# An edge pass re-cut as a pipeline of nine turns, with nine buffers of gathered rows

## The chip, the cores and the metric

The kernel runs on one core of a Trainium2 chip. The metric is device time in microseconds from one launch to its end; the time before is the median of three runs, 9715.59 us (9711.79 to 9739.76). One core has several engines that run their own instruction streams side by side and wait for one another through semaphores: TensorE (PE, matrix products and transposes), VectorE (DVE), ScalarE (ACT), GpSimd (POOL, which here issues the indirect gathers) and SyncE (SP, which here issues plain loads). Matrix products land in PSUM; everything else of the kernel's working data lies in SBUF.

## What is computed

Two graph layers, each added to its input and normalized. There are 12,500 nodes with 64 features and 400,000 edges, sorted by their target node. The first layer takes means over neighbours twice. The second, which the change touches, turns each edge's 64 attributes into a weight vector by two small linear maps with a softplus after each, multiplies it with the row of the edge's source node, and sums over the edges of each target:

```python
def _L1_gnn_ref(node_feats_in, edge_feats, src, dst, Wn, bn, We1, be1, We2, be2, Wc, bc, Wp, bp):
    LOG2 = float(np.log(2.0))
    def ssp(x):
        return jax.nn.softplus(x) - LOG2
    V = node_feats_in.shape[0]
    h = node_feats_in @ Wn.T + bn
    h_src = h[src]
    w = ssp(edge_feats @ We1.T + be1)
    w = ssp(w @ We2.T + be2)
    m = h_src * w
    agg = jax.ops.segment_sum(m, dst, num_segments=V)
    out = ssp(agg @ Wc.T + bc)
    return out @ Wp.T + bp
...
x = _layernorm(x + _L0_gnn_ref(x, edge_index, ...), axis=-1)
x = _layernorm(x + _L1_gnn_ref(x, edge_attr_64, src, dst, ...), axis=-1)
```

## The kernel before

The kernel runs in stages, one after the other: two passes over the edges for the first layer (up to about 4,400 us in the profile), small per-node networks, then **pass three** for the second layer (about 4,690 to 9,385 us), then the last per-node networks. The change touches pass three only.

Pass three cuts the 400,000 edges into 391 groups: 390 of 1,024 edges (T = 8 slots of 128 edges) and a last one of five slots. The loop over windows at L888 runs once on this data. What one group needs, by the names that the profile shows:

- `got`: the source nodes' rows, 64 floats each. `gather` (L849) has GpSimd issue eight indirect gathers (L853) of 128 rows. A buffer of `got` holds one group; there are eight.
- `att`: the edges' attributes, 256 KB, loaded by SyncE (L931) into one of four buffers. TensorE turns them by four transposes into `m_t` (PSUM, L935), ScalarE copies that to `m_at` (L937).
- First map: TensorE `m_1` (L954; the profile calls both maps' results `m`). VectorE adds the bias and clips into `m_v` (`under`, L911), ScalarE takes Exp and Ln (L915, L916), VectorE takes the larger of that and the unclipped value (`larger`, L919).
- Second map: TensorE `m_2` (L948), and the same chain again into `m_w`.
- TensorE turns `m_w` back by four transposes into `m_b` (L941), VectorE multiplies with the gathered rows into `m_m` (L944). This is the last reader of the group's `got` buffer.
- VectorE makes `same` (L860), a 0/1 matrix that says which of 128 neighbouring target nodes each edge belongs to; TensorE sums with it over the edges into `p_sum` (eight products, L868); VectorE adds `p_sum` into its place in `acc` (L886), at an address loaded into a register.

The program is written out in full for all groups; the order in which the groups' steps stand in it is the order in which each engine runs them. Before, it is a pipeline of three groups: in step k the newest group k is gathered, turned and put through the first map, group k−1 goes through the second map and `compare`, and group k−2 is turned back, multiplied, summed and placed:

```python
new = groups[k] if k < len(groups) else None
mid = groups[k - 1] if 0 < k <= len(groups) else None
old = groups[k - 2] if k > 1 else None
```

So within one step, work goes from TensorE to the other engines and back several times: `m_t` to `m_at` to `m_1` to `m_v`, for instance, all belong to one step of one group. The multiply of group k−2 frees the buffer into which group k+6 is gathered. In PSUM, `p_sum` has two buffers, and `m_t`, `m_b`, `m_1`, `m_2` have one each. `same` and `got` live in the pool "esb" (L839), `p_sum` in "eps", the rest in pools that `message_pools` makes (L894).

Of the kernel before, what the change touches and what calls it, by code (L numbers as in the profile page):

```python
# [9 lines left out]
F32 = mybir.dt.float32  # L10
# [40 lines left out]
T = 8  # L51
ET = P * T
W = 128
NG = E // ET
# [13 lines left out]
def gnn_kernel(ctx, tc, x, src, dst, ea, W_lin, b_lin, W1_agg, W1_root, b1, W2_agg, W2_root, b2,  # L68
               Wn, bn, We1, be1, We2, be2, Wc, bc, Wp, bp, out):
    nc = tc.nc  # L70
# [13 lines left out]
    ident = const.tile([P, P], F32, name="ident")  # L84
# [5 lines left out]
    with tc.tile_pool(name="ints", bufs=1) as sb:  # L90
        n = sb.tile([P, KB * P + DW], I32, name="n")
# [5 lines left out]
    eps = const.tile([P, 1], F32, name="eps")  # L97
# [23 lines left out]
    turned = []  # L121
    with tc.tile_pool(name="wps", bufs=2, space=PSUM) as wps, tc.tile_pool(name="given", bufs=1) as given_:
        for w, name in ((Wn, "wn"), (We1, "we1"), (We2, "we2"), (Wc, "wc"), (Wp, "wp")):
            given = diagonal([(0, 0, w)], F, name + "_given", given_)
            pt = wps.tile([P, P], F32, name="pt")
            nc.tensor.transpose(pt, given, ident)
            t = const.tile([P, P], F32, name=name)
            nc.vector.tensor_copy(t, pt)
            turned.append(t)
    wn, we1, we2, wc, wp = turned  # L130
# [19 lines left out]
    be1_c, be2_c = less_log2(column(be1, "be1_c")), less_log2(column(be2, "be2_c"))  # L150
# [73 lines left out]
    with tc.tile_pool(name="prep", bufs=1) as sb, tc.tile_pool(name="prepps", bufs=1, space=PSUM) as ps:  # L224
# [10 lines left out]
        with tc.tile_pool(name="ints2", bufs=1) as sb2:  # L235
            n = sb2.tile([TP, TJ], I32, name="n")
            nc.gpsimd.iota(n, pattern=[[1, TJ]], base=0, channel_multiplier=TJ)
            nc.vector.tensor_scalar(real, n, float(DT), None, op0=ALU.is_lt)
            n = sb2.tile([P, NB], I32, name="n_ids")
# [45 lines left out]
        start = sb.tile([P, NGG + 1], F32, name="start")  # L285
# [15 lines left out]
        g = sb.tile([P, (NGG + 1) * T], I32, name="g")  # L301
# [71 lines left out]
    with tc.tile_pool(name="n0", bufs=2) as sb, tc.tile_pool(name="n0x", bufs=1) as sx, \  # L373
# [3 lines left out]
        for c in range(NCH):  # L377
            cs = slice(c * CH, (c + 1) * CH)
            k = CH // 2
            xt = pairs_turned(ps, sb, xs[:, cs, :].rearrange("p (k j) f -> p k (j f)", j=2), k, P, "xt")  # L380
            ph = ps.tile([P, 1024], F32, name="ph")
            for b, m in banks(k):
                nc.tensor.matmul(ph[:, b * P:(b + m) * P], wlin, xt[:, b * P:(b + m) * P],
                                 start=True, stop=True)
# [3 lines left out]
            for j in range(k):  # L388
                nc.tensor.matmul(py[:, j * 4 * H:(j + 1) * 4 * H], ht[:, j * P:(j + 1) * P], w1,
                                 start=True, stop=True)  # L390
# [332 lines left out]
    with tc.tile_pool(name="n1", bufs=2) as sb:  # L723
        for c in range(NCH):
# [5 lines left out]
            m = sb.tile([P, CH, H], F32, name="m1")  # L730
            nc.vector.tensor_tensor(m, s[:, :, :H], rdeg[:, cs].unsqueeze(2).to_broadcast([P, CH, H]),
                                    op=ALU.mult)
# [15 lines left out]
    with tc.tile_pool(name="n2", bufs=2) as sb, tc.tile_pool(name="n2ps", bufs=1, space=PSUM) as ps, \  # L748
# [33 lines left out]
        for c in range(NCH):  # L782
            cs = slice(c * CH, (c + 1) * CH)
            k = CH // 2
# [34 lines left out]
    windows = nc.values_load(count[0:1, 0:1], min_val=1, max_val=N // W + 1)  # L819


    big = ctx.enter_context(tc.tile_pool(name="big", bufs=1))
    cps = ctx.enter_context(tc.tile_pool(name="cps", bufs=1, space=PSUM))
    acc = big.tile([F, NA], F32, name="acc")
# [4 lines left out]
    e_att = ea[:NG * ET, :].rearrange("(g p t) f -> g p t f", p=P, t=T)  # L829
    l_att = ea[NG * ET:, :].rearrange("(p t) f -> p t f", t=TL)  # L830

    def edge_pass(stages, pools):

        nc.vector.memset(acc, 0.0)
        nc.vector.tensor_copy(base, first)
        with ExitStack() as st:
            sb = st.enter_context(tc.tile_pool(name="esb", bufs=3))  # L839
            ps = st.enter_context(tc.tile_pool(name="eps", bufs=2, space=PSUM))  # L840
            work = pools(st)
            at = {}

            class Group:
                def __init__(self, g):
                    self.g, self.n = g, T if g < NG else TL
                    self.got = None

                def gather(self):  # L849
                    self.got = sb.tile([P, T, F], F32, name="got", bufs=8)  # L850
                    for t in range(self.n):
                        c = self.g * T + t
                        nc.gpsimd.indirect_dma_start(  # L853
                            out=self.got[:, t, :], out_offset=None, in_=t3[:, :],
                            in_offset=bass.IndirectOffsetOnAxis(ap=srcs[:, c:c + 1], axis=0))

                def compare(self):
                    n = self.n
                    self.same = sb.tile([P, T, W], F32, name="same")
                    nc.vector.tensor_tensor(  # L860
                        self.same[:, :n, :], across(steps[:, :W], [P, n, W]),
                        rel[:, self.g * T:self.g * T + n].unsqueeze(2).to_broadcast([P, n, W]),
                        op=ALU.is_equal)

                def gathered_sum(self, m):
                    self.p = ps.tile([F, W], F32, name="p_sum")
                    for t in range(self.n):
                        nc.tensor.matmul(self.p, m[:, t, :], self.same[:, t, :],  # L868
                                         start=t == 0, stop=t == self.n - 1)

                def place(self):
                    g = self.g
                    if g % 8 == 0:
                        k = min(8, NG + 1 - g)
                        loads, v = nc.values_load_multi_w_load_instructions(
                            base_i[0:1, g:g + k], engines=(mybir.EngineType.DVE,), min_val=0, max_val=NP,
                            skip_runtime_bounds_check_because="a base is a node's number, held at NP or "
                            "less where it moves, and acc has W columns more", bass_reorder=False)
                        at.update({g + i: v[i] for i in range(k)})
                        if g:  # L880
                            for load in loads:
                                tc.add_manual_dep(load.ins, at["last"].ins.name, mybir.DependencyInfo(
                                    mybir.DependencyClass.NoSync, mybir.DependencyReason.DATA),
                                    reason="in order")
                    here = acc[:, ds(at[g], W)]
                    at["last"] = nc.vector.tensor_tensor(here, self.p, here, op=ALU.add)  # L886

            with tc.For_i(0, windows, 1):  # L888
                nc.vector.tensor_copy(base_i, base[0:1, :])
                stages(work, [Group(g) for g in range(NG + 1)])  # L890
                nc.vector.tensor_scalar(base, base, float(W), float(NP), op0=ALU.add, op1=ALU.min)
                nc.vector.tensor_scalar(rel, rel, -float(W), None, op0=ALU.add)

    def message_pools(st):  # L894
        return (st.enter_context(tc.tile_pool(name="msb", bufs=2)),
                st.enter_context(tc.tile_pool(name="mps", bufs=1, space=PSUM)))

    def log_part(sb, v, bias, w, name):

# [3 lines left out]
        nc.scalar.activation(a[:, :w], a[:, :w], AF.Ln, bias=half)  # L903
        return a[:, :w]

    def second(work, groups):
        sb, ps = work

        def under(g, p, bias, name):
            a = sb.tile([P, 512], F32, name=name)  # L910
            nc.vector.tensor_scalar(a, p, bias, TOP, op0=ALU.add, op1=ALU.min)  # L911
            return a

        def logs(a):
            nc.scalar.activation(a, a, AF.Exp)  # L915
            nc.scalar.activation(a, a, AF.Ln, bias=half)  # L916

        def larger(a, p, bias):
            nc.vector.scalar_tensor_tensor(a, p, bias, a, op0=ALU.add, op1=ALU.max)  # L919

        nc.scalar.preload_act_table_set("natural_log_exp_and_others")
        for k in range(len(groups) + 2):
            new = groups[k] if k < len(groups) else None
            mid = groups[k - 1] if 0 < k <= len(groups) else None
            old = groups[k - 2] if k > 1 else None
            if new:
                new.gather()
                new.att = sb.tile([P, T, F], F32, name="att", bufs=4)
                if new.n < T:
                    nc.gpsimd.memset(new.att, 0.0)  # L930
                nc.sync.dma_start(new.att[:, :new.n, :], e_att[new.g] if new.g < NG else l_att)  # L931
                pt = ps.tile([P, 512], F32, name="m_t")
                flat = new.att.rearrange("p t f -> p (t f)")
                for j in range(0, 512, P):
                    nc.tensor.transpose(pt[:, j:j + P], flat[:, j:j + P], ident)  # L935
                at = sb.tile([P, 512], F32, name="m_at")
                nc.scalar.copy(at, pt)  # L937
            if old:
                pb = ps.tile([P, 512], F32, name="m_b")
                for j in range(0, 512, P):  # L940
                    nc.tensor.transpose(pb[:, j:j + P], old.w[:, j:j + P], ident)  # L941
                n = old.n
                old.m = sb.tile([P, T, F], F32, name="m_m")
                nc.vector.tensor_tensor(old.m[:, :n, :], pb.rearrange("p (t f) -> p t f", f=F)[:, :n, :],  # L944
                                        old.got[:, :n, :], op=ALU.mult)
            if mid:
                mid.p2 = ps.tile([P, 512], F32, name="m_2")
                nc.tensor.matmul(mid.p2, we2, mid.v, start=True, stop=True)  # L948
                mid.w = under(mid, mid.p2, be2_c, "m_w")
                logs(mid.w)  # L950
                mid.compare()
            if new:
                new.p1 = ps.tile([P, 512], F32, name="m_1")
                nc.tensor.matmul(new.p1, we1, at, start=True, stop=True)  # L954
                new.v = under(new, new.p1, be1_c, "m_v")
            if mid:
                larger(mid.w, mid.p2, be2_c)
            if new:
                logs(new.v)
                larger(new.v, new.p1, be1_c)  # L960
            if old:
                old.gathered_sum(old.m)
                old.place()

    edge_pass(second, message_pools)


    def store(c, y):
# [69 lines left out]
```

## Time and profile before

| | us |
|---|---|
| median of three runs (lowest, highest) | 9715.59 (9711.79, 9739.76) |
| the profiled execution's own time | 9518.89 |
| its span, first to last instruction | 9517.1 |
| mean granted TensorE clock, share of full speed | 0.682 |

The page's busy time by engine, and the costliest group on ScalarE in pass three:

```profile
PE 5181.2 (54%) x28141; PEld 2897.6 (30%) x28141; DVE 4064.2 (43%) x11900; ACT 2257.4 (24%) x3480; POOL 5264.9 (55%) x5503
...
L915 ACT ACTIVATE m_w<-m_w 128x512 f32<-128x512 f32 x391 | 246.3, 630 | 3085.0 <-DVE m_w L911 2680.9
```

In the first line each engine has its busy microseconds, their share of the span and its number of instructions; PEld is the loading of weights into TensorE, which overlaps its products. In the second, a line of the page's list of groups: line, engine, operation, output and input, how many; then busy us in total, mean ns of one, and the idle time of the engine just before them, with what ended most of it. ScalarE's 3,085 us of idle time there say only that ScalarE has little to do; what matters is whose idle time sets the pace. "remote" as a releaser means that the page found no instruction that ended the wait, and "issue" that nothing shown was waited for. Durations of matrix products on TensorE are modelled, not observed to their end.

### The profile page before, as it was taken

The page shows a single profiled execution, that of the slowest core. Times are in us where ns is not written, and L with a number is a line of the kernel's source. Part 1 is how long each engine was busy: PE and PEld are TensorE (multiplying, and loading weights), DVE is VectorE, ACT ScalarE, POOL GpSimd, SP SyncE. Part 2 cuts the span into 40 slices and gives each one's busy share as a digit, 9 for nine tenths or more (in the row PEclk, how much of TensorE's full clock was granted, in tenths as well). Part 3 has the DMA queues.
Part 4 walks back from the last instruction along what each step waited for, and adds up shares of the span by engine and source line. Part 5 has one row for each costly group of instructions (what it writes and reads, how often), then busy time and mean ns, then how long its engine had stood idle before and what let it go on. Part 6 is the DMA issues. An engine that isn't in the chain of part 4 may idle for free.

```text
span 9517.1 us, 85323 instructions
## 1 busy us (share of the span) xinstructions
PE 5181.2 (54%) x28141; PEld 2897.6 (30%) x28141; DVE 4064.2 (43%) x11900; ACT 2257.4 (24%) x3480; POOL 5264.9 (55%) x5503
## 2 busy tenths in 40 slices
PE   2677777777723334344445555555555555555555
PEld 1233333333312222223323333333333333333333
DVE  2566667667611111111533444444344444444445
ACT  0333334334300000000122222222222222222224
POOL 0555455555266555654266666666666666666661
PEclk9566566666655555556567777777777777777777
DMA  2233333333343434344211111111111111111110
GB/s 46 92 119 118 118 118 118 118 118 123 136 153 123 143 134 158 133 161 164 66 38 44 45 45 45 45 45 46 45 45 44 44 46 45 44 45 45 45 45 25
DMA packets 403898, 791.32 MB, mean 83 GB/s; under 512 B 149567, under 2 KB 193439, under 8 KB 403197
## 3 DMA queue, kind: packets, MB, share of 16 engines
q1 hardware_dynamic: 207737, 632.94, 18.3%
q0 software_dynamic: 176032, 143.83, 8.2%
q10 hardware_dynamic: 19653, 8.71, 0.4%
q8 instruction: 237, 3.88, 0.2%
q14 instruction: 239, 1.96, 0.1%
HBM read 516.47 MB, written 268.57 MB: 82 GB/s over the span
## 4 chain that ended last, share of the span: by engine, by line
another core or an unknown queue 15%; PE 11%; issue 10%; DVE 8%; POOL 4%; ACT 3%; DMA 1%; DVEq 0%; POOLq 0%; ACTq 0%
POOL got L853 4%; PE m L948 4%; PE p_sum L868 2%; PE m L954 2%; DVE m_v L919 2%; DVE m_m L944 1%; DVE same L860 1%; ACT m_w L915 1%; DVE m_w L911 1%; DMA got<-t,srcs 1%; ACT m_at L937 1%; ACT m_w L916 1%; DVE m_w L919 1%; PE m_b L941 1%
## 5 line engine op out<-in xcount | busy, mean ns | idle before, releaser
L853 POOL DMA_INDIRECT got<-t,srcs x3125 | 2960.7, 947 | 1888.8 <-issue 819.8
L436 POOL DMA_INDIRECT got<-sent,gidx x2346 | 2277.4, 971 | 1862.8 <-PE p_got L450 850.0
L948 PE MATMUL m<-m_v,we 128*128 128x512 f32 x782 | 629.5, 898 | 1543.0 <-DVE m_v L919 1149.3
L516 PE MATMUL p_counts<-to,lo 128*128 128x392 bf16 x2560 | 1028.9, 463 | 503.4 <-DVE to L515 220.0
L525 PE MATMUL p_sums<-counts,addends 128*64 128x256 bf16 x7840 | 1078.5, 368 | 369.2 <-issue 273.3
L518 ACT CAST counts<-p_counts 128x784 bf16<-128x784 f32 x1120 | 890.8, 813 | 1157.4 <-PE p_counts L516 668.2
L868 PE MATMUL p_sum<-same,m_m 128*64 128x128 f32 x6250 | 923.5, 310 | 281.6 <-DVE m_m L944 281.5
L868 PEld LDWEIGHTS p_sum<-same,m_m 128*64 128x64 f32 x6250 | 820.4, 159 | 731.8 <-DVE m_m L944 491.6
L915 ACT ACTIVATE m_w<-m_w 128x512 f32<-128x512 f32 x391 | 246.3, 630 | 3085.0 <-DVE m_w L911 2680.9
L450 PE MATMUL p_got<-got,same 128*128 128x51 bf16 x4692 | 434.3, 215 | 890.5 <-DVE s_new L417 545.5
L515 DVE TENSOR_SCALAR to<-ramp,keys 128x392 bf16<-128x392 f16 x2560 | 828.0, 323 | 1.8 <-DVE lo L513 1.3
L525 PEld LDWEIGHTS <-addends 128*64 128x64 bf16 x7840 | 525.2, 137 | 829.1 <-issue 716.2
L886 DVE TENSOR_TENSOR acc<-p_sum,acc 64x128 f32 x391 | 109.9, 281 | 1439.7 <-remote 1310.1
L513 DVE TENSOR_SCALAR lo<-ramp,keys 128x128 bf16<-128x128 f16 x2560 | 651.3, 254 | 165.5 <-PE p_counts L516 74.5
L948 PEld LDWEIGHTS m<-m_v,we 128*128 128x128 f32 x782 | 157.5, 251 | 1630.2 <-DVE m_v L919 1203.5
L417 DVE TENSOR_REDUCE s_new<-p_got 128x34 f32<-128x102 f32 x294 | 77.5, 264 | 1324.2 <-remote 969.6
L450 PEld LDWEIGHTS <-same 128*128 128x128 bf16 x4692 | 286.7, 112 | 1100.8 <-issue 656.9
L516 PEld LDWEIGHTS <-lo 128*128 128x128 bf16 x2560 | 271.0, 107 | 1054.3 <-DVE to L515 512.7
L944 DVE TENSOR_TENSOR m_m<-m_b,got 128x512 f32<-128x512 f32 x391 | 267.3, 684 | 747.4 <-remote 395.7
L954 PE MATMUL m<-m_at,we 128*128 128x512 f32 x782 | 577.8, 832 | 0.7 <-ACT m_at L937 0.7
L444 DVE TENSOR_SCALAR same<-ramp,grel 128x256 bf16<-128x256 f16 x2346 | 518.0, 296 | 139.7 <-remote 127.2
L601 ACT COPY rs<-p_sums 128x256 f32<-128x256 f32 x80 | 29.9, 373 | 1980.2 <-PE p_sums L525 958.5
(258 smaller groups left out, 5235.7 us busy)
## 6 DMA issues: line engine op xcount, KB each, us to landing
kept<-counts SPq DMA_DIRECT2D x280, 896.0 KB
counts<-kept SPq DMA_DIRECT2D x560, 448.0 KB
att<-in_edge_attr_dram SPq DMA_DIRECT2D x390, 256.0 KB
got<-t,srcs POOLq DMA_INDIRECT x3125
got<-sent,gidx POOLq DMA_INDIRECT x2346
t<-h SPq DMA_DIRECT2D x7, 448.0 KB
xs<-in_x_dram ACTq DMA_DIRECT2D x6, 448.0 KB
xs<-in_x_dram SPq DMA_DIRECT2D x6, 448.0 KB
```

Of the source, the lines that this page charges most:

```text
L436: nc.gpsimd.indirect_dma_start(out=got[i][:, t, :], out_offset=None, in_=sent[step][:, :], in_offset=bass.IndirectOffsetOnAxis(ap=gidx[:, ...
L444: nc.vector.tensor_scalar(same[:, t, :], ramp[:, :KG * P], grel[:, i * T + t:i * T + t + 1], None, op0=ALU.is_equal)
L450: nc.tensor.matmul(p[:, k * SW:(k + 1) * SW], same[:, t, k * P:(k + 1) * P], rows[:, t, :SW], start=t == 0, stop=t == n - 1)
L513: nc.vector.tensor_scalar(lo, ramp[:, :P], keys[:, 1, i:i + 1], None, op0=ALU.is_equal)
L515: nc.vector.tensor_scalar(to, ramp[:, :MW], keys[:, 0, i:i + 1], None, op0=ALU.is_equal)
L516: nc.tensor.matmul(p[:, k, :MW], lo, to, start=True, stop=True)
L518: copy(counts[:, :, q * 2 * DW:(q + 1) * 2 * DW].rearrange("p h (k d) -> p h k d", k=2), p[:, :, :MW].rearrange("p k (d h) -> p h k d", h= ...
L525: nc.tensor.matmul(p[r:r + YW, :HI * DW], addends[:, h, :], counts[:, h - of, :], start=h < 2, stop=h >= NPP - 2)
L853: nc.gpsimd.indirect_dma_start(out=self.got[:, t, :], out_offset=None, in_=t3[:, :], in_offset=bass.IndirectOffsetOnAxis(ap=srcs[:, c:c + ...
L868: nc.tensor.matmul(self.p, m[:, t, :], self.same[:, t, :], start=t == 0, stop=t == self.n - 1)
L948: nc.tensor.matmul(mid.p2, we2, mid.v, start=True, stop=True)
L954: nc.tensor.matmul(new.p1, we1, at, start=True, stop=True)
```

## The change

Pass three is written as a pipeline of nine turns. In turn k the helper `at(back)` gives group k − back, or nothing at the ends, and each turn does one step for each of nine groups: gathers and the first transposes for group k, the copy and the first map for k−1, the chain after the first map for k−2, the second map for k−3, the chain after it for k−4, the transposes back for k−5, the multiply for k−6, `compare` and the sums for k−7, and `place` for k−8. Attributes are loaded two turns ahead of use. In the text of a turn the steps of ScalarE and VectorE stand ahead of those of TensorE. There are eight turns more than groups, where there were two.

Buffers: `got` nine instead of eight; `att` five instead of four; `same` two instead of three; the `m_...` tiles in SBUF three instead of two; in PSUM `m_1` and `m_2` two instead of one, `p_sum` one instead of two. The number and the shapes of the instructions per group stay as they are.

```diff
-    def edge_pass(stages, pools):
+    def edge_pass(stages):
...
-            ps = st.enter_context(tc.tile_pool(name="eps", bufs=2, space=PSUM))
-            work = pools(st)
+            ps = st.enter_context(tc.tile_pool(name="eps", bufs=1, space=PSUM))
...
-                    self.got = sb.tile([P, T, F], F32, name="got", bufs=8)
+                    self.got = sb.tile([P, T, F], F32, name="got", bufs=9)
...
-                    self.same = sb.tile([P, T, W], F32, name="same")
+                    self.same = sb.tile([P, T, W], F32, name="same", bufs=2)
...
-    def message_pools(st):
-        return (st.enter_context(tc.tile_pool(name="msb", bufs=2)),
-                st.enter_context(tc.tile_pool(name="mps", bufs=1, space=PSUM)))
...
+        def turned(p, a):
+            for j in range(0, 512, P):
+                nc.tensor.transpose(p[:, j:j + P], a[:, j:j + P], ident)
+
+        def attributes(g):
+            g.att = sb.tile([P, T, F], F32, name="att", bufs=5)
+            if g.n < T:
+                nc.gpsimd.memset(g.att, 0.0)
+            nc.sync.dma_start(g.att[:, :g.n, :], e_att[g.g] if g.g < NG else l_att)
+
+        def multiply(g):
+            n = g.n
+            g.m = sb.tile([P, T, F], F32, name="m_m")
+            nc.vector.tensor_tensor(g.m[:, :n, :], g.pb.rearrange("p (t f) -> p t f", f=F)[:, :n, :],
+                                    g.got[:, :n, :], op=ALU.mult)
...
-        for k in range(len(groups) + 2):
...
+        for g in groups[:2]:
+            attributes(g)
+        for k in range(len(groups) + 8):
+            def at(back):
+                return groups[k - back] if 0 <= k - back < len(groups) else None
+            if g := at(0):
+                g.gather()
+            if g := at(-2):
+                attributes(g)
+            if g := at(1):
+                g.at = sb.tile([P, 512], F32, name="m_at")
+                nc.scalar.copy(g.at, g.pt)
+            if g := at(2):
+                g.v = under(g.p1, be1_c, "m_v")
+                logs(g.v)
+            if g := at(6):
+                multiply(g)
+            if g := at(4):
+                g.w = under(g.p2, be2_c, "m_w")
+                logs(g.w)
+            if g := at(8):
+                g.place()
+            if g := at(7):
+                g.compare()
+            if g := at(2):
+                larger(g.v, g.p1, be1_c)
+            if g := at(4):
+                larger(g.w, g.p2, be2_c)
+            if g := at(3):
+                g.p2 = ps.tile([P, 512], F32, name="m_2", bufs=2)
+                nc.tensor.matmul(g.p2, we2, g.v, start=True, stop=True)
+            if g := at(5):
+                g.pb = ps.tile([P, 512], F32, name="m_b")
+                turned(g.pb, g.w)
+            if g := at(7):
+                g.gathered_sum()
+            if g := at(0):
+                g.pt = ps.tile([P, 512], F32, name="m_t")
+                turned(g.pt, g.att.rearrange("p t f -> p (t f)"))
+            if g := at(1):
+                g.p1 = ps.tile([P, 512], F32, name="m_1", bufs=2)
+                nc.tensor.matmul(g.p1, we1, g.at, start=True, stop=True)
```

More of the change, by code (lines that the diff above doesn't have):

```diff
@@ L863, in compare, with gathered_sum @@
                         op=ALU.is_equal)
-                def gathered_sum(self, m):
+                def gathered_sum(self):
                     self.p = ps.tile([F, W], F32, name="p_sum")
                     for t in range(self.n):
-                        nc.tensor.matmul(self.p, m[:, t, :], self.same[:, t, :],
+                        nc.tensor.matmul(self.p, self.m[:, t, :], self.same[:, t, :],
                                          start=t == 0, stop=t == self.n - 1)
@@ L889, in edge_pass @@
                 nc.vector.tensor_copy(base_i, base[0:1, :])
-                stages(work, [Group(g) for g in range(NG + 1)])
+                stages(sb, ps, [Group(g) for g in range(NG + 1)])
                 nc.vector.tensor_scalar(base, base, float(W), float(NP), op0=ALU.add, op1=ALU.min)
                 nc.vector.tensor_scalar(rel, rel, -float(W), None, op0=ALU.add)
-    def message_pools(st):
-        return (st.enter_context(tc.tile_pool(name="msb", bufs=2)),
-                st.enter_context(tc.tile_pool(name="mps", bufs=1, space=PSUM)))
     def log_part(sb, v, bias, w, name):
@@ L904, in log_part, with second, under @@
         return a[:, :w]
-    def second(work, groups):
-        sb, ps = work
-        def under(g, p, bias, name):
+    def second(sb, ps, groups):
+        def under(p, bias, name):
             a = sb.tile([P, 512], F32, name=name)
@@ L919, in larger @@
             nc.vector.scalar_tensor_tensor(a, p, bias, a, op0=ALU.add, op1=ALU.max)
-        nc.scalar.preload_act_table_set("natural_log_exp_and_others")
-        for k in range(len(groups) + 2):
[L923 to L963, printed above, removed]
@@ L965, in gnn_kernel @@
-    edge_pass(second, message_pools)
+        def turned(p, a):
[11 more added lines that the diff above has]
+                                    g.got[:, :n, :], op=ALU.mult)
@@ L968, in store @@
+    edge_pass(second)
     def store(c, y):
```

## The prediction, made before the changed kernel was run

> **What bounds the kernel now.** I read the page first, for the groups with the longest idle time; then the waits between 5000 and 9300 us (the body of pass three, which is all the change touches); then the windows, for the pace; then the timelines of one typical cycle on VectorE and TensorE.
>
> Page, costliest groups (busy us, mean ns, idle before and its releaser):
> ```profile
> L853 POOL DMA_INDIRECT got<-t,srcs x3125 | 2960.7, 947 | 1888.8 <-issue 819.8
> L886 DVE TENSOR_TENSOR acc<-p_sum,acc 64x128 f32 x391 | 109.9, 281 | 1439.7 <-remote 1310.1
> L944 DVE TENSOR_TENSOR m_m<-m_b,got 128x512 f32<-128x512 f32 x391 | 267.3, 684 | 747.4 <-remote 395.7
> ```
> Waits, 5000 to 9300 us (total us, times, longest):
> ```profile
> DVE acc L886 <- remote: 1175.6, 170, 12.4
> POOL got L853 <- issue: 756.6, 2479, 0.6
> POOL got L853 <- DVE m_m L944: 741.6, 191, 7.8
> DVE m_m L944 <- remote: 372.1, 74, 8.5
> ```
> Windows (length, then PE, PEld, DVE, ACT, POOL busy, granted clock, DMA share, GB/s); the last one, after the final gather, is cut at 9344 to 9381:
> ```profile
> 5000.00:6000.00 1000.00, 539.99 (x2352) 332.03 (x2352) 407.71 (x587) 251.97 (x420) 633.48 (x672) 0.76 0.19 44
> 6000.00:7500.00 1500.00, 817.76 (x3531) 506.29 (x3531) 613.50 (x885) 378.22 (x632) 953.09 (x1011) 0.75 0.19 45
> 7500.00:9340.00 1840.00, 1008.50 (x4367) 618.50 (x4368) 762.31 (x1092) 468.58 (x779) 1172.84 (x1244) 0.76 0.19 45
> 9344.00:9381.00 37.00, 27.68 (x155) 17.73 (x154) 27.79 (x41) 15.33 (x25) 0.00 (x0) 1.00 0.00 1
> ```
> No engine is busy: POOL, the busiest, has 64%. Its 2759.41 us in the three long windows are 2759.41 / 0.947 = 2,914 gathers, or 364 groups of eight, in 4,340 us: **11.92 us per group**. The gathers alone need less. They start every 1.2475 us (0.94 and the 0.30 of "issue"), so eight take 9.98 us. The missing 1.94 us is POOL's wait for the multiply m_m (741.6 us in 191 waits, 3.9 each, about one in every two groups).
>
> One cycle on POOL and VectorE (idle before, releaser in brackets):
> ```profile
> 7018.32 0.94 POOL L853 DMA_INDIRECT got<-t,srcs  x1 [3.96 <-DVE m_m L944]
> ...
> 7037.03 0.94 POOL L853 DMA_INDIRECT got<-t,srcs  x1 [0.30 <-issue]
> 7041.90 0.94 POOL L853 DMA_INDIRECT got<-t,srcs  x1 [3.92 <-DVE m_m L944]
> ```
> ```profile
> 7023.28 0.67 DVE L944 TENSOR_TENSOR m_m<-m_b,got 128x512 f32<-128x512 f32 x1
> ...
> 7032.51 0.28 DVE L886 TENSOR_TENSOR acc<-p_sum,acc 64x128 f32 x1 [4.64 <-remote]
> 7032.72 1.21 DVE L860 TENSOR_TENSOR same<-steps,rel 128x1024 f32<-128x1024 f32 x1
> 7033.85 0.73 DVE L919 SCALAR_TENSOR_TENSOR m_v<-m,be_c,m_v 128x512 f32<-128x512 f32 x1
> 7040.93 0.69 DVE L944 TENSOR_TENSOR m_m<-m_b,got 128x512 f32<-128x512 f32 x1 [6.36 <-remote]
> ```
> And on TensorE:
> ```profile
> 7025.32 1.96 PE L868 MATMUL p_sum<-same,m_m 128*64 128x128 f32 x16
> 7027.21 0.66 PE L935 MATMUL m_t<-ident,att 128*128 128x128 f32 x4
> 7028.01 0.63 PE L941 MATMUL m_b<-ident,m_w 128*128 128x128 f32 x4
> ```
> Here is the point of the whole reading. By its records p_sum is done at 7027.28, yet the addition that needs it starts at 7032.51. m_b is done at 7028.64, yet the multiply starts at 7040.93. "remote" means that the page found no releaser; the trace's own list of semaphore updates has TensorE's next ones at 7032.48, 7039.48 and 7040.91, so VectorE really waited for **late completions of TensorE**. The rhythm repeats: two groups' multiplies free two buffers, POOL runs sixteen gathers, TensorE's second p_sum comes late, POOL runs out of buffers, and some 3 us after its last gather (7037.97 to 7040.91) everything held back completes at once. The first p_sum of a cycle is prompt: over 4900 to 9300 us one that ends 3 to 4 us after POOL's restart is used 0.04 us later (median of 79), one that ends 9 to 10 us after it 7.5 us later (60). In the tail, with no gather running, a multiply comes every 6.3 to 6.5 us without such a wait. So the bound is TensorE's completions while POOL streams gathers. Why streaming gathers hold them back the trace does not say.
>
> **What the Trainium skill says.** "Perfetto Trace Analysis", section on the per-instruction lifecycle: TensorE's end is estimated from the instruction's size, and the semaphore goes out only when PSUM acknowledges the bytes. The trace agrees: 7027.28 against 7032.48. The same section: a software-generated DMA's profiled end is the end of descriptor generation, not of the transfer; so the 3 us between POOL's last gather and the release include its landing. "Trainium Kernel Development and Optimization", Best Practices, tells one to double-buffer so that transfers overlap computation; this trace, with eight buffers, shows that overlap can itself be what goes with late completions.
>
> **The change, part by part.**
> *Instructions.* Nothing is added or removed per group: 8 gathers, 7 VectorE, 5 ScalarE operations, 56 TensorE instructions (32 p_sum, 8 m_t, 8 m_b, 4 each for m_1 and m_2), one attribute load. Cost 0.
>
> *Order.* By the built program a turn is, on VectorE: m_v under, m_m, m_w under, acc, same, both larger; on TensorE: p_sum, m_2, m_1, m_b, m_t. Everything VectorE reads was made in the turn before, except one thing: p_sum needs the `same` of its own turn, and m_2, m_1, m_b, m_t queue behind p_sum. The next turn's first VectorE operation waits for that m_1, and the multiply behind it for m_b. The loop is therefore serial. VectorE to the end of `same`, by start-to-start times in the cycle above and its row: 0.66 + 0.61 + 0.66 + 0.21 + 1.21 = 3.35. TensorE: p_sum 1.96, m_2 and m_1 0.95 each: 3.9, at this cycle's warm clock; the next pair of m records (2.07, 1.91 long) shows about double when cold. A turn takes 7.3 us warm, up to 11 cold, against 6.4 before. It fits under POOL's 9.98 when warm, with 2.7 us for late completions; those seen are 5 to 12 us late.
>
> *Buffers of rows, 8 to 9.* Before, the multiply of group k−2 frees the buffer of k+6; now that of k−9 runs in turn k−3. POOL's lead falls from six groups to three. POOL uses up all buffers in either kernel, so the lead buys nothing by itself.
>
> *Attributes two turns early, five buffers.* No wait on them is in the list of waits. Gain 0; without that cover an issue would show on m_t. *One PSUM buffer for p_sum instead of two*: acc(k−8) stands ahead of `same` on VectorE, so it is read before p_sum(k−7) starts; 0, at most acc's 0.28 per turn.
>
> *Steady cycle.* If completions are still held while POOL streams, sixteen gathers end 19.65 us after the first, the release comes at 22.6 (7018.32 to 7040.91). Before, the multiply was next on VectorE, and POOL restarted 0.97 after its start: 23.58. Now m_v under stands ahead of it (0.66): 24.24, so 12.12 us a group for this cycle, 0.33 more than its 11.79. Some earlier cycles, where VectorE had acc and `same` to do before the multiply after the release, lose that work, so I take +0.28 on the mean 11.92: **12.2**. Over some 380 groups: +106. Below: 11.7 if those cycles are common (−84); above: 12.8, see the fourth rival (+346 at 12.83).
>
> *Ends.* The drain has eight turns more than groups instead of two, and POOL stops with nine buffers full: after the last gather some 11 turns of 7.5 are left, 82 us, where now 49 pass (9337 to 9385.4): +33. The first multiply comes in the seventh turn instead of the third: four turns of 7.5 to 10, less one more buffer of 10 us for POOL: +20 to +30. Together +60 (between +35 and +115).
>
> *Sum.* +106 + 60 = +166 on the profiled execution: 9518.9 (span 9517.1) to 9,685. The median of the runs, 9715.6, stands 197 above that execution; where the 197 lies isn't shown, so I add the difference unscaled: **9,882, say 9,880 us**.
>
> **Rivals.**
> 1. *POOL becomes the bound* (not slower). Late completions are a matter of who waits in which order, and a whole turn of slack hides them. Then 391 × 9.98 = 3,902, plus fill 60 and drain 82, is 4,044 against 4,695 (4690 to 9385): −650, 9,065. For it: the tail runs freely, and 7.3 is under 9.98. Against: the loop has 2.7 us of slack and delays are larger; and in pass three's first uninterrupted stretch, 80 gathers from 4702 to 4801, completions came only 5.6 to 11.2 us apart.
> 2. *Three groups per stop* (not slower). If turns of 7.3 put a third multiply ahead of POOL's stop: 23 × 1.2475 + 0.94 + 2.95 + 1.63 = 34.2 for three, 11.4 each: −198 + 60 = −138, 9,578. For it: m_1 and m_2 ending 8 us after the restart still passed promptly. Against: p_sum ending then did not, and it leads each turn.
> 3. *The hold costs per unit of work, not per order*: pace 11.9 as now, ends hidden in part: +0 to +60, 9,745. For it: the same 56 instructions.
> 4. *Only one multiply per restart.* It decides once a turn takes longer than 9.98 us from multiply to multiply: at a cold clock (11) or with one late m_1 or m_b. POOL then stops after eight gathers (9.67), release +2.95, restart +1.63: 14.25. All cycles so: +885 + 60, 10,660. Every second cycle: (14.25 + 24.24) / 3 = 12.83, +346 + 60, 10,122. For it: 8-gather stretches exist already, 12 of them. Against: they are few, and the first turn after a restart has been prompt.
>
> **How the numbers follow.** Forecast (two groups per stop) 0.47, own range 9,700 to 10,020 (−84 with +60, to a quarter of the cycles single); rival 1 0.16, rival 2 0.15, rival 3 0.12, rival 4 0.10. The range 9,540 to 10,130 leaves out rival 1 and half of rival 4. About 0.3% (29 us) is what a measurement tells from no change: faster 0.32 (rivals 1 and 2 and the low end of the forecast), within 0.10 (half of rival 3, little of the forecast), slower 0.58.
>
> **What will show it.** Right: POOL still in stretches of sixteen gathers with stops of 4 to 5 us "← DVE m_m"; the long remote waits gone from acc and moved to the first operation of the turn, m_v under; 12.2 us a group. Rival 1: stops gone, POOL near 76% busy. Rival 2: stretches of 24. Rival 4: stretches of eight. The forecast fails if TensorE's completions, in the new order, are no longer late while POOL streams.

## The result, and the profile after

| | before | after |
|---|---|---|
| median of 18 runs each, us | 9695.8 | 9752.65 |
| lowest to highest | 9667.71 to 9739.76 | 9724.0 to 9779.8 |
| ratio after to before, 95% interval | | 1.0056 (1.0044 to 1.0067) |
| span of the profiled execution | 9517.1 | 9751.1 |

The changed kernel is slower by 0.56%, 57 us at the medians. The forecast had slower and +166 us: the sign held, the size was three times too large.

Runs were made in *sessions*, each with runs of the kernel before beside it, and the sessions came in two kinds, called here *held* (the kernel before takes 9,519 to 9,786 us; the comparison above is of this kind) and *free* (7,918 to 7,972 us), so times are compared within a session only, or as ratios to the kernel before of the same session.

The waits of the changed kernel, same columns and window as in the prediction:

```profile
ACT m_at L945 <- remote: 2290.7, 181, 23.0
DVE acc L886 <- remote: 1794.7, 161, 24.4
...
POOL got L853 <- DVE m_m L928: 889.5, 162, 9.2
```

The long remote waits are still there. They did not move to the first operation of the turn, as forecast; they grew on acc (1,794.7 against 1,175.6 us), and ScalarE's copy of m_t, which waits for TensorE too, now has long ones as well. POOL stops less often (162 times against 191) and longer (5.5 us each against 3.9). One such stop, first on POOL and then on VectorE:

```profile
7010.29 0.95 POOL L853 DMA_INDIRECT got<-t,srcs  x1 [0.30 <-issue]
7019.79 0.94 POOL L853 DMA_INDIRECT got<-t,srcs  x1 [8.55 <-DVE m_m L928]
```
```profile
6985.19 0.67 DVE L928 TENSOR_TENSOR m_m<-m_b,got 128x512 f32<-128x512 f32 x1
...
6990.18 0.69 DVE L928 TENSOR_TENSOR m_m<-m_b,got 128x512 f32<-128x512 f32 x1 [0.35 <-PE p_sum L868]
6990.79 0.74 DVE L905 TENSOR_SCALAR m_w<-m,be_c 128x512 f32<-128x512 f32 x1
7015.53 0.28 DVE L886 TENSOR_TENSOR acc<-p_sum,acc 64x128 f32 x1 [24.00 <-remote]
7015.74 1.21 DVE L860 TENSOR_TENSOR same<-steps,rel 128x1024 f32<-128x1024 f32 x1
7016.87 0.73 DVE L913 SCALAR_TENSOR_TENSOR m_v<-m,be_c,m_v 128x512 f32<-128x512 f32 x1
7017.53 0.73 DVE L913 SCALAR_TENSOR_TENSOR m_w<-m,be_c,m_w 128x512 f32<-128x512 f32 x1
7018.19 0.73 DVE L905 TENSOR_SCALAR m_v<-m,be_c 128x512 f32<-128x512 f32 x1
7018.85 0.67 DVE L928 TENSOR_TENSOR m_m<-m_b,got 128x512 f32<-128x512 f32 x1
```

Three multiplies come in quick succession, the last two 5.0 us apart, and free three buffers; POOL then runs 24 gathers without a pause. The p_sum that ended by its records at 6989.99 is used at 7015.53, 4.3 us after the last gather's end (7011.24). Then five operations (3.3 us) stand ahead of the multiply that lets POOL go on. Between 5000 and 9500 us POOL ran 8 gathers at a stretch 27 times, 16 gathers 83 times and 24 gathers 56 times, where the kernel before has nearly always 16. A stretch with its stop takes 16.8, 23.0 and 38.2 us at the median: 16.8, 11.5 and 12.8 us per group. What the good cycles win the others lose.

The window that was counted before:

```profile
6000.00:7500.00 1500.00, 732.21 (x3356) 519.86 (x3356) 563.30 (x840) 373.61 (x600) 911.34 (x966) 0.72 0.19 43
```

911.34 / 0.947 / 8 is 120.3 groups in 1,500 us, 12.47 us each; over 5000 to 9340, counted as in the prediction, 12.48, against the 11.92 of the profiled execution before. But that execution, at 9518.9 us, was unlike the 18 runs, of which the fastest took 9667.7. So the first question was what the kernel before looks like in another execution.

### The profile page after: what moved, and what is told of

The parts are those of the page before. It is cut to its first block, busy times and chain, and to the rows that moved or that the text cites. A ratio compares the mean times of both kernels' runs of the same rounds, so it can differ in the third digit from the quotient of the medians.

```text
span 9751.1 us, 84557 instructions
## 1 busy us (share of the span) xinstructions
PE 5086.4 (52%) x28141; PEld 3054.7 (31%) x28141; DVE 3997.8 (41%) x11900; ACT 2300.5 (24%) x3480; POOL 5261.7 (54%) x5503
## 4 chain that ended last, share of the span: by engine, by line
another core or an unknown queue 23%; PE 12%; DVE 7%; issue 6%; POOL 2%; ACT 2%; DMA 1%; DVEq 0%; SPq 0%; ACTq 0%; POOLq 0%
PE p_sum L868 6%; DVE same L860 2%; PE m L964 2%; POOL got L853 2%; PE m L975 2%; DVE m_w L905 1%; PE m_t L917 1%; DVE m_m L928 1%; DVE m_v L913 1%; DMA got<-t,srcs 1%; DVE m_v L905 1%; PE m_b L917 1%; DVE m_w L913 1%; DVE acc L886 0%
## 5 line engine op out<-in xcount | busy, mean ns | idle before, releaser
L868 PE MATMUL p_sum<-same,m_m 128*64 128x128 f32 x6250 | 1107.4, 352 | 1187.0 <-DVE same L860 983.4
L868 PEld LDWEIGHTS p_sum<-same,m_m 128*64 128x64 f32 x6250 | 990.4, 184 | 1291.5 <-DVE same L860 1032.9
L945 ACT COPY m_at<-m_t 128x512 f32<-128x512 f32 x391 | 228.0, 583 | 3245.6 <-remote 2555.9
L917 PE MATMUL m_t<-ident,att 128*128 128x128 f32 x1564 | 314.1, 329 | 980.3 <-issue 634.9
L917 PEld LDWEIGHTS m_t<-ident,att 128*128 128x128 f32 x1564 | 215.8, 167 | 1029.8 <-issue 665.7
L964 PE MATMUL m<-m_v,we 128*128 128x512 f32 x782 | 518.6, 749 | 20.2 <-DVE m_v L913 14.2
```

What stands on the lines that cost most here:

```text
L868: nc.tensor.matmul(self.p, self.m[:, t, :], self.same[:, t, :], start=t == 0, stop=t == self.n - 1)
L917: nc.tensor.transpose(p[:, j:j + P], a[:, j:j + P], ident)
L964: nc.tensor.matmul(g.p2, we2, g.v, start=True, stop=True)
```

## Experiments

In the labels of the runs, a_ stands for the changed kernel with one edit, b_ for the kernel before with one edit, and a number at the end for a repeat.

**1. The same two kernels again (no edit).** After the first session (number 2 below), which turned out to be of the free kind:

> The kernel before, unchanged, profiled a second time. The four runs ahead of this one ran on a chip on which the kernel before took 7955.68 us, 1,740 us less than in the comparison (9695.8). Theory 1c (whether TensorE's completions are held back is a property of the chip, not of the kernel): on a chip with 7,950 to 8,000 us the trace has POOL streaming without stops, pass three at 9.98 us per group and no long remote waits, its stages ahead of pass three shorter as well; on a chip near 9,700 us stretches of sixteen gathers and 11.8 to 12.4 us per group. Rival (the time varies from launch to launch on any chip): times in between.

> The changed kernel, unchanged, on the same chip as before_2. Theory 1c: on a chip near 7,950 us both kernels stand at POOL's 9.98 us per group, and the changed one is slower by its longer fill and drain alone, 40 to 70 us. On a chip near 9,700 us: as in the comparison, 9,720 to 9,780 us, with irregular stretches of 8, 16 and 24 gathers. Rival 1 of the prediction (the pipeline hides late completions) would have it faster than the kernel before on a chip that holds them.

Measured: a held session, the kernel before 9,786.4 us (and 9,726.5 in the run beside it), the changed one 9,749.6. The profiled 9,786.4 lies above all 18 runs of the comparison, as 9,518.9 lies below them. The kernel before, profiled for the second time:

```profile
6000.00:7500.00 1500.00, 732.22 (x3362) 449.02 (x3361) 588.65 (x840) 363.97 (x600) 904.58 (x959) 0.74 0.17 42
```
```profile
DVE acc L886 <- remote: 1550.9, 161, 14.5
...
POOL got L853 <- DVE m_m L944: 902.1, 187, 7.4
```

904.58 where the first profile had 953.09. Over 5000 to 9340 this execution takes **12.50 us per group**, the changed kernel 12.48. Its stretches are the same 16 gathers, but their usual period is 25.4 us instead of 23.6. The pace of the kernel before thus ranges from 11.9 to 12.5 with no change in the code, and the new order stands at the upper end of that range. Pass three, from the first gather to the last addition, took 4,696.5 and 4,914.3 us in these two profiles, and 4,887.5 and 4,889.3 in two of the changed kernel (after and after_2).

**2. No gathers, plain loads, other work on POOL.** Four kernels in one session. Edits: `gather` takes a fixed tile of ones (no gathers); or

```diff
-                        nc.gpsimd.indirect_dma_start(
-                            out=self.got[:, t, :], out_offset=None, in_=t3[:, :], ...)
+                    r = (self.g * P * T) % (N - P * T)
+                    nc.sync.dma_start(self.got[:, :self.n, :],
+                                      t3[r:r + P * self.n, :].rearrange("(t p) f -> p t f", p=P))
```

or, in place of each gather, `nc.gpsimd.tensor_copy(self.got, fixed)`.

> The kernel before with pass three's gathers left out: the multiply reads a fixed tile of ones, so the output differs. Theory 1 (TensorE's completions are held back only while POOL streams gathers): no long remote waits on acc or m_m, 6.3 to 6.5 us per group as in the tail of the kernel before, pass three near 2,500 us, total near 7,500 us. Rival (the late completions belong to TensorE itself, its clock or its order): long remote waits remain, 10 to 12 us per group, total 9,000 to 9,700 us.

> The changed kernel with pass three's gathers left out (fixed tile of ones, output differs). By the prediction's step (serial loop) a turn takes 7.3 us, pass three near 2,900 us. By the reading of the trace after, in which m_v's first operation didn't wait for the m_1 behind p_sum, a turn takes 4.5 to 5.5 us, pass three near 2,000 us and the total near 7,000 us. If the late completions are TensorE's own, 10 to 12 us per group.

> The changed kernel with the same bytes in the same 256-byte pieces, loaded by SyncE in one plain load per group (neighbouring rows, so the output differs), none by POOL. Theory 1a (it is POOL's making of descriptors, or its software queue, that holds TensorE's completions): as fast as without gathers, 4.5 to 6 us per group, total near 7,000 to 7,300 us. Theory 1b (it is the small-packet traffic): late completions remain, 10 us per group or more, total over 8,800 us.

> The changed kernel with the gathers replaced by eight copies on POOL that fill the same buffers from a tile of ones (no transfer, output differs). If any streaming work of POOL holds TensorE's completions, stretches of POOL work and long remote waits on acc as in the changed kernel, 12 us per group or more. If it takes descriptors or transfers, none of these waits; then a group takes the longer of the turn (4.5 to 5.5 us) and POOL's eight copies.

Measured: totals 6,553.8, 5,917.7, 5,916.9 and 6,073.2 us, beside 7,955.7 of the kernel before: a free session, so these say nothing on the late completions, and POOL's copies were not tried in a held one. They do measure the two orders by themselves: **6.45 us per group before, 4.84 after**, 5.25 with POOL's copies. The new order is far the better one when neither gathers nor late completions bound it. One turn of the changed kernel on TensorE, gathers left out:

```profile
4999.56 1.12 PE L961 MATMUL m<-m_v,we 128*128 128x512 f32 x2
5000.53 1.02 PE L972 MATMUL m<-m_at,we 128*128 128x512 f32 x2
5001.39 0.60 PE L914 MATMUL m_b<-ident,m_w 128*128 128x128 f32 x4
5002.22 0.55 PE L914 MATMUL m_t<-ident,att 128*128 128x128 f32 x3 [0.24 <-ACT m_at L942]
5002.70 1.96 PE L865 MATMUL p_sum<-same,m_m 128*64 128x128 f32 x16
5004.59 1.13 PE L961 MATMUL m<-m_v,we 128*128 128x512 f32 x2
```

TensorE goes from product to product, 98% busy. p_sum is the *last* step of a turn. In the prediction I took it for the first.

**3. Plain loads in a held session (same kernel as a_plain).** A first repeat was in a free session (a_plain_2, 5,932.2 us); the second:

> a_plain for a chip that holds completions. If software gathers are what holds them: 4.8 us per group, pass three 1,900 us, and the passes ahead of it as long as in the comparison (pass three begins near 4,730 us), total near 6,800 us. If small-packet traffic is: over 8 us per group, total over 8,000 us.

Measured: 6,786.4 us beside 9,740.05, a held session. Pass three runs at the free pace there too; its window and what is left of VectorE's wait for p_sum:

```profile
5000.00:6500.00 1500.00, 1464.32 (x8668) 1030.23 (x8667) 1416.85 (x2166) 979.11 (x1546) 0.00 (x0) 1.00 0.43 109
```
```profile
DVE acc L884 <- PE p_sum L866: 43.1, 41, 1.1
```

The DMA share is 0.43 against 0.19 in the gathers' pass, and no completion is late: the longest wait is 1.1 us. The packets are smaller, too. The page's list of queues (packets, MB, share of 16 engines), for the changed kernel and for this one:

```profile
q1 hardware_dynamic: 207737, 632.94, 17.8%
q0 software_dynamic: 176032, 143.83, 8.7%
```
```profile
q1 hardware_dynamic: 613993, 735.36, 32.6%
q0 software_dynamic: 76032, 41.23, 3.5%
```

The gathers are 100,000 packets in the software queue, half of them of 2,048 bytes (eight rows) and half of 4; the plain loads that take their place are 406,256 packets in the hardware queue, 400,000 of 256 bytes and the rest of 4. So neither busy DMA engines nor small packets hold TensorE's completions; leaving out the software gathers ends the hold. What it is about the gathers this does not say. The two kernels also differ in that there is one load per group instead of eight gathers, with 16 packets of 4 bytes instead of 128, and in that the rows are neighbours instead of scattered; no run separates these.

**4. Paced gathers.** A small fill on POOL behind every gather of pass three, tied into the order:

```diff
+                        behind(nc.gpsimd.memset(scrap[:, :256], 0.0))
```

`behind` adds an ordering without a semaphore. Widths 1, 160, 256 and 400 gave cadences of 1.249, 1.361, 1.441 and 1.561 us. The first session:

> The changed kernel with one fill of 128x1 on POOL behind every gather of pass three, in program order; the gathers' cadence grows from 1.2475 us by some tenth of a microsecond, 0.1 to 0.3. Theory 2 (on a chip that holds completions, something serves each gather in about 1.4 us, POOL issues one every 1.25, the surplus piles up and TensorE's completions wait behind it; both passes with a bound of gathers there show 1.48 to 1.57 us per gather overall): paced near 1.4 us the pile hardly grows, stretches are longer than 24 gathers or unbroken, and a group takes 11.2 to 12 us instead of 12.45: pass three 150 to 450 us shorter. Rival (the hold follows from POOL streaming at all, whatever its pace): the stops stay as long as they are and the fills come on top, 12.9 to 14 us per group. On a chip that holds nothing: 8 x cadence per group, slower than the kernel before by 0.1 to 0.3 x 3125.

> As a_pace1 with a fill of 128x256, so a longer pause: cadence 1.4 to 1.7 us. Theory 2: at a cadence over 1.5 us no pile at all, acc's long remote waits gone, POOL without stops, and a group takes 8 x cadence. Rival (any streaming holds): stops remain and the time per group is that of the changed kernel plus the fills.

> The kernel before with the same fill as a_pace1. Theory 2: the same gain as a_pace1 within 0.3 us per group, since the order of the other engines' work isn't what sets the pace. If the nine-turn order tolerates late completions better than the old one, a_pace1 gains and this doesn't.

Measured: 7,936.4, 8,549.9 and 7,962.2 us beside 7,965.3: a free session, and so no test. The 128x1 fill (0.118 us) vanishes in the 0.30 us that stand between two gathers anyway. Then the same a_pace2 in the held session of number 3:

> a_pace2 once more, for a chip that holds completions (the kernel before near 9,700 us there; near 7,960 us this run only repeats 8,550). Cadence 1.441 us, 11.53 us per group if nothing stops POOL. Theory 2 (a pile that grows because POOL issues faster than something serves): few or no stops, 11.5 to 12 us per group, 150 to 370 us less than the changed kernel, which stands at 12.45. Rival (streaming holds at any pace): stops remain, 13 us per group or more, 200 us more than the changed kernel.

Measured: **9,462.5 us beside 9,740.05, a ratio of 0.972** (one run of each, no interval). Its waits, 5000 to 9200 us:

```profile
DVE acc L895 <- remote: 1338.7, 278, 8.2
...
POOL got L861 <- DVE m_m L937: 4.0, 3, 2.3
```

POOL's wait for the multiply has shrunk to 4.0 us in three times. POOL streams for hundreds of gathers, at 11.56 us per group, about eight times its cadence. TensorE's completions are still late: VectorE waits for p_sum 278 times, 4.8 us each, but at most 8.2, never 24. The pipeline hides most of this, not all: over this window the multiplies come 11.8 us apart, so POOL's lead grows, from 1.1 groups at the first multiply to 8.4 at 7167 us, until the nine buffers are nearly used up. Gathers 0.19 us further apart, 0.9 us less per group of POOL's pace: the rival that foresaw the stops to stay and 13 us per group is out.

> b_pace2, timed, for a chip that holds completions: within 60 us of a_pace2_2 (9,460) if the order of the work does not set the pace once the gathers are paced; over 9,800 us, with stops, if the nine-turn order is what makes late completions harmless. Near 8,570 on a chip that holds nothing.

Two earlier runs of this kernel were in free sessions (8,563.4 and 8,588.9 us). This one was held, though of a milder kind (the kernel before 9,531.1, seven runs): 9,386.9 us, **a ratio of 0.9853 (0.9829 to 0.9877)**. From the first gather to the last addition pass three took 4,554 us here and 4,587 in a_pace2_2, and the same 11.56 us per group:

```profile
5000.00:9200.00 4200.00, 2504.32 (x10124) 1774.56 (x10124) 1743.04 (x2535) 1082.20 (x1809) 3710.96 (x5816) 0.79 0.18 46
```
```profile
DVE m_m L953 <- DMA got<-t,srcs: 1915.2, 362, 6.6
...
DVE acc L895 <- PE p_sum L877: 96.7, 164, 1.3
```

The multiply waits for its rows now, which is how a pass bound by its gathers looks, and no remote wait is left on acc. So the old order, too, runs at POOL's pace once the gathers are spaced: with paced gathers the order does not set the pace. That no completion is late here, while they are in a_pace2_2, can be owed to the order or to the milder session; the two were changed together.

> The changed kernel with a fill of 128x160 behind every gather: cadence near 1.36 us, 10.9 us per group if nothing stops POOL. On a chip that holds completions, theory 2 with a service time between 1.25 and 1.36 us: no stops, pass three near 4,300 us, total near 9,230 us, 230 less than a_pace2_2. With a service time between 1.36 and 1.44: stops come back, total 9,300 to 9,600. Rival (any streaming holds, and a_pace2_2 gained for another reason): 9,750 or more. On a chip that holds nothing: 3125 x 0.11 more than the changed kernel, near 8,290.

> The changed kernel with a fill of 128x400: cadence near 1.56 us, 12.45 us per group. On a chip that holds completions, theory 2: the delay of p_sum, 4.1 us in the mean in a_pace2_2, falls to under 1 us, since TensorE's completions get the time that the gathers leave free, and the total is near 9,790 us (a_pace2_2 plus 0.114 x 3125 = 356, less nothing). If the delay is a fixed cost of any gather beside TensorE it stays near 4 us.

Both were in a free session: 8,293.1 us (ratio 1.0435, 1.0417 to 1.0452) and 8,931.6 beside 7,945.6. Where nothing is held, each pause simply costs itself. (The delay of p_sum that this last expectation goes by, from its end to acc, would not have told lateness alone: it is 5.4 us in the free run after_3 below, where VectorE waits for rows first.) Where between 1.249 and 1.441 us the stops begin was not measured in a held session.

**5. The change where nothing is held (no edit).**

> The changed kernel, unchanged, timed against the kernel before on this chip. On a chip that holds nothing: POOL bound in both, 10.03 us per group; the changed kernel is 15 to 35 us shorter than the kernel before, by its shorter end after the last gather (10 against 27 us in a_pace1 and b_pace1, whose fills cost nothing at 1.249 us). On a chip that holds completions: 30 to 80 us longer, as in the comparison.

Measured, a free session: 7,932.8 against 7,946.5 us, **ratio 0.9976 (0.9965 to 0.9988)**. There the changed kernel is faster, by 14 us at the medians. Both are bound by POOL (9.99 to 10.03 us per group). From the last gather's end to the last addition it takes 9 us here and 27 in b_pace1, which has the old order at the same cadence. These 18 us are no less than the whole difference.

**A theory that fell.** I held the difference between sessions for a property of the chip (1c). The chips' numbers go against it: two sessions bear the same number, and one was free (a_pace3), the other held (b_pace2_3). The pass just ahead, untouched by the change, shows the kind as well: its gathers come every 1.57 to 1.59 us on average in held sessions and every 1.25 in free ones. What makes a session held stays open, and so does what TensorE's completions queue behind. Theory 2, a pile that grows because gathers are issued faster than something serves them, fits the pacing and the releases (about 3 us after 16 gathers, 4.3 after 24), but no run shows that something.

Two things in the traces narrow it. The rows themselves do not pile up: counted off at 16 per gather, a gather's last data packet ends 1.2 us after the gather in the profile after, at the first as at the 24th gather of a stretch, and 1.1 us in the free after_3. And semaphore updates are missing from the traces of held sessions, just where gathers run: between 5000 and 9200 us the profile after has 1,583 of VectorE's 2,402 and some 10,800 of the 48,700 that the transfers should make, counted at 16 each. The free after_3 (4000 to 7700 us) has all of VectorE's 2,637 and over 99% of the transfers'; so has a_plain_3 between 4900 and 6500 us, in a held session but without gathers. So the updates, or the profiler's recording of them, may be what backs up; no run tested either. Gaps alone don't make completions late, though: b_pace2_3 has them as well (2,011 of VectorE's 2,580).

## Why the prediction was right in sign and wrong in size

The step that failed is "The loop is therefore serial": a turn takes 4.84 us, not 7.3. With it fell the ends, forecast at +60 and measured at about −14, which is 74 of the 109 us that the forecast was too high. The same reading put the stop at m_v; since p_sum ends the turn, acc is the first on VectorE to wait. The second failure is the steady cycle with its baseline: neither the stop nor the 11.92 us per group that it was added to was the usual one. That the sign came out right is in part luck, since the forecast stop (two groups, at m_v) is not the one that occurred.

- **"TensorE's completions while POOL streams gathers" as the bound: right.** Shown by a_plain_3 (gathers gone, waits gone); the two paced runs agree. The trace's list of TensorE's semaphore updates, on which the reading leaned, has gaps (1,227 of 1,772 between 5000 and 9200 us), but VectorE's starts say the same.
- **The instructions, cost 0, and the buffers, "the lead buys nothing": consistent.** Both kernels ran at the same pace when held, and at POOL's when free; the buffers alone were not tried.
- **"The loop is therefore serial", 7.3 us warm: wrong, 4.84 measured.** TensorE's stream repeats without a mark where a turn begins. I cut it ahead of p_sum and so made m_1 and m_b of a turn wait for p_sum of the same turn. The real turn ends with p_sum.
- **"Steady cycle", 24.2 us for two groups, taken as 12.2 per group: 12.48 measured.** Not two groups per stop but a mix of one, two and three; p_sum was used first among the late ones, so the stop fell on acc, with 3.3 us of VectorE work after it instead of 0.66. The second rival (three groups per stop) happened in a third of the stretches, at 38.2 us and not 34.2: the release came after 4.3 us instead of 2.95, and the same 3.3 us followed.
- **"The median stands 197 above that execution; I add the difference unscaled": the step that hid the most.** The 197 lay mostly in the very term that I was estimating: of the 268 us between the two profiles of the kernel before 218 lie in pass three, and the second runs at 12.50 us per group, not 11.92. Against 11.92 the steady term would be +0.56 per group; against 12.50 it is −0.02.
- **"Ends", +60: measured about −14.** From the last gather's end to the last addition 35 and 41 us in two profiles after, 49 and 56 in two before; from the first gather to the first multiply 28 against 27. Of the 11 turns that were to follow the last gather 10 and 11 did, but at some 3.5 us each, not 7.5. Eight more turns cost little when a turn is short, so this follows from the serial loop.

Put together as an estimate: if the pace of the kernel before lies between its two profiles as its time does, its median of 9,695.8 goes with 12.30 us per group (66% of the way from 9,518.9 to 9,786.4). Then the steady term is 0.18 x 391 = +70, and with −14 at the ends +56, against +57 measured. The agreement is better than the estimate, which rests on two profiles that both lie outside the 18 runs: the same interpolation lets pass three begin 7 us later in the changed kernel, though nothing ahead of it was changed. Against the second profile alone the steady term is nothing and pass three is 25 us shorter after the change, so that the steady term is above nothing is not shown. By this estimate the forecast's steady +106 came out near 70 by two errors that partly cancel: both the pace before and the pace after were put too low. The third rival, that the hold goes with the work and not with its order, describes the outcome best. One difference between two sessions helps to read it: the profile at 9518.9 resembles the milder held session of b_pace2_3, in which the kernel before took 9,518.9 to 9,558.1 us; the changed kernel was not run in such a session.

## What to carry to other kernels

Before pricing a change against a profile, check that the profiled execution is like the timed ones; when it is 2% off, a second profile tells more than any sum. When producer and consumer share a bound that is neither's own busy time, reordering the consumer moves the stops about, while spacing the producer can remove them: gathers 0.19 us further apart took 1.5 to 2.8% off where completions were held, and cost 7.3 to 8.1% where they were not, so it pays only if one knows which of the two one has. And to read a pipeline's loop, find in the trace where a turn begins on each engine before adding up what waits for what.

## What the runs showed of the hardware

In a held session a product's end in the trace can stand 25 us ahead of its completion (6989.99 against 7015.53), while over the last 17 us of these POOL's gathers, until 7011.24, are all that looks busy on the engines. Plain loads of as many bytes, in smaller packets and at more than twice the DMA share, delayed nothing (longest wait for p_sum 1.1 us). The traces of held sessions lack part of the semaphore updates while gathers run. And the same program on the same data took 9,519 to 9,786 us or 7,918 to 7,972, each session keeping to one of the two.
